# Weighing and scoring attention pair by pair, with the flags' reductions and first weight sums at other places

## The chip, the cores and the metric

The kernel runs on one core of a Trainium2 chip. A core has TensorE (PE, matmuls; its weight loads are shown as PEld), VectorE (DVE), ScalarE (ACT), GpSimd (POOL) and SyncE (SP, which here only issues DMAs). Each engine takes its instructions in the order in which the program lists them, and waits on semaphores for what others make. The metric is the device time of one execution in microseconds (us).

## The reference, cut to what matters

64 graphs of 256 nodes, 512 features each, pass through two layers of masked attention. All arithmetic is in float32.

```python
h = relu(layernorm(x))                       # layer 0: 4 heads of 64
q, k, v = h @ Wq, h @ Wk, h @ Wv
sim = where(adjacency, q @ k.T * 64**-0.5, -max)
x = x + softmax(sim) @ v @ Wo + bo
h = relu(layernorm(x))                       # layer 1: 8 heads of 64
h = layernorm(h) * gamma + beta
q, k, v = split(h @ w_qkv.T)
scores = where(adjacency | eye, q @ k.T * 64**-0.5, -1e9)
x = x + softmax(scores) @ v @ w_out.T + b_out
```

A node of layer 0 without any neighbour has all its scores masked alike, and its softmax is uniform. That is why the kernel needs a flag for each node, whether it has a neighbour at all: the maximum over its row of the adjacency.

## The kernel before, in words

**Steps and units.** Two graphs make a step; there are 32 (`NSTEP`). Heads go in pairs, since two heads of 64 fill 128 partitions. Layer 0 has the pairs 0 and 1 (called L0), layer 1 has 0 and 2 (L1A) and 1 and 3 (L1B). A set of two pairs is handled together.

**Matmuls of projections.** Every large product is cut into 2 x 2 blocks and done in 7 block products instead of 8. It needs sums of weight blocks (`weight_sum`, made once, at the start) and of activation blocks (`act_sums0`, `act_sums1`, on POOL). The products come in the order 1, 6, 5, 2, 7, 3, 4 (or 1, 5, 2, 6, 7, 3, 4). Products 2, 4 and 3 accumulate into the PSUM bank in which 1, 7 and 5 were left (`SHARED`), so they wait until that bank has been read. After each product VectorE or ScalarE takes the bank over (`evacuate`, L745 and on; `accumulate`, L764 and on).

**PSUM.** Eight banks: four with the name `sc` (pool `ps_sc`), and four `mm` banks, which `mm_tile` hands out in turn, the least recently used first, leaving out those held for a later product.

**A visit.** `visit(period, w, prev, cur)` is the piece of attention that stands between two blocks of projections. For the pairs of `prev`, `weigh_out` multiplies the exponentials by the values (L1041, 128x32 tiles of the array, four at a time), and ScalarE copies the result out (L1056). For the pairs of `cur`, `scores` makes the scores (L970, 64x128 tiles, two at a time), VectorE adds the mask while it moves them out (`mask_scores`, L993), and ScalarE takes exponentials (L998). Later POOL adds the two key halves (`key_halves`, L1005), VectorE turns and reduces them (L1011, L1018, `turn_sums` L1071, `key_sums` L1079 to L1083), the inverses go through DRAM by SP (L1089, L1100), and POOL multiplies the weighed values by them (`normalise`, L1116). With W for the weighing of a pair and S for its scores, TensorE does W0, W1, S0, S1. W0 and W1 write `sc` banks; S0 writes four `sc` banks; S1 writes two `mm` and two `sc` banks.

**The order.** It is written out by hand. `at(period, place, fn, ...)` files a piece of work under a number, period times 6.4 plus place, and at the end all pieces are sorted by it. Each engine gets its instructions in that order. `at_set` spreads the seven products of a projection over a length of one; a product's evacuation is filed just ahead of the next product. A period of the steady state, for step s:

| place | TensorE |
|---|---|
| 0.0 | queries and keys of L1A (`project_qk`, L817) |
| 1.0 | `combine` of layer 1 of the step before (L914) |
| 2.0 (`AT_X`) | visit X: weighs layer 0 of the next step, scores L1A |
| 2.0 | values of layer 1 (`project_v1`, L898); adjacency turned (L563) |
| 3.0 | `combine` of layer 0 of the next step (L914) |
| 3.5 | queries and keys of L1B (L817) |
| 4.5 (`AT_Q0`) | visit Q0: weighs L1A, scores L1B |
| 4.5 | queries and keys of layer 0, two steps ahead (L817) |
| 5.5 (`AT_V0`) | values of layer 0, turned (`project_v0_turned`, L864) |
| 6.2 (`AT_Z`) | visit Z: weighs L1B, scores layer 0 |

**Work beside it.** The adjacency flags are made by `neighbours` (VectorE, maximum, L521), `neighbours_line` (VectorE, four small transposes into one row, L530) and `neighbours_spread` (three DMAs from SP that copy the row, L537). `norm0` and `norm1` take the moments (L590, L591); POOL makes the scales (`row_scales`, L600 to L602); ScalarE applies them (L606). The normalised h is turned by VectorE in 32 x 32 blocks (`turn_blocks`, L700), moved by 16 DMAs (`move_blocks`, L712) and placed by ScalarE (`place_h`, L723 for layer 0, L725 for layer 1). The values of layer 0 are turned by `turn_values` (VectorE, L878) into a tile that `place_h` of layer 1 has to have read, and moved by ScalarE's queue (L888).

**x and its tiles.** The residual x of a step is loaded in two halves by ScalarE's queue (`load_graph`, L502) into one of two tiles, gets its biases from POOL (`first_bias` L508, `second_bias` L652), and is stored in two halves (`store_graph`, L948), the first graph by ScalarE's queue, the second by SP's. A tile is loaded anew only when both halves of the step before the last are stored. The load is filed at X + 0.005 and X + 0.025, the first pair's exponentials at X + 0.02 and X + 0.03.

Of the kernel before, what the change touches and what calls it, by code (L numbers as in the profile page):

```python
# [8 lines left out]
FP = mybir.dt.float32  # L9
# [306 lines left out]
def fast_path(  # L316
# [19 lines left out]
    nc = tc.nc  # L336
    P = 128
    B, N, D = x.shape
    DH = 64
    G = 2  # L340
    NSTEP = B // G
# [689 lines left out]
            st["oT0"] = flat[:, :NB].rearrange("p (b c) n -> p b c n", c=HP0)  # L1031
            st["invb"] = [flat[:, 8:10], flat[:, 10:12]]

    def weigh(s, lyr, pr):
        st = S[s]
        p = st["p", lyr, pr]
        po = ps_sc.tile([P, G, N], FP, name="sc")
        for g in range(G):
            for kc in range(NIC):
                for r0 in range(0, P, 32):  # L1040
                    nc.tensor.matmul(  # L1041
                        po[r0:r0 + 32, g, :],
                        (
                            st["v1"][:, g * NIC + kc, pr * P + r0:pr * P + r0 + Q] if lyr else
                            st["v0"][:, r0 // Q, pr, g * NIC + kc, :]
                        ),
                        p[r0 // DH][:, g, kc, :], start=(kc == 0), stop=(kc == NIC - 1),
                    )
        half = (HP0, HP1)[lyr]
        b0, b1, step = B_OF[pr // half]  # L1050
        dst = st[f"oT{lyr}"][:, b0:b1:step, pr % half, :]
        return po, dst

    def weigh_out(s, lyr, pr):
        po, dst = weigh(s, lyr, pr)
        nc.scalar.copy(dst, po)  # L1056
        S[s]["dst", lyr, pr] = dst

    def weigh_last(pr):

        po, dst = weigh(NSTEP - 1, 1, pr)
        nc.vector.tensor_tensor(dst, po, S[NSTEP - 1]["invb", 1, pr], ALU.mult)

    def turn_sums(s, lyr, prs):
# [78 lines left out]
    def visit(period, w, prev, cur):  # L1143

        w -= 0.0003
        s, lyr, prs = prev
        last = (s, lyr) == (NSTEP - 1, 1)
        if prs:
            if prs[0] == 0 and not last:
                at(period, w - 0.0002, place_values, s, lyr)  # L1150
            if (s, lyr) == (1, 0):
                turned = sums = 0, 0.88
            elif 0 <= period < NSTEP - 2 and s > 0:
                sums = turned = (
                    (period, AT_X + 1.45) if abs(w - AT_Q0) < 0.01 else
                    (period, AT_V0 + 0.5595) if abs(w - AT_Z) < 0.01 else (period - 1, AT_Z + 1.25)
                )
                if abs(w - AT_Z) < 0.01:
                    turned = period, AT_V0 + 0.41
            else:  # L1160
                turned = sums = period, w - 0.0001
            at(*turned, turn_sums, s, lyr, prs)
            at(*sums, key_sums, s, lyr, prs)
            at(period, w - 0.00008, inverse_in, s, lyr, prs)
            for i, pr in enumerate(prs):
                if not last:
                    at(period, w, weigh_out, s, lyr, pr)
                    at(period, w + (0.55 if len(prs) == 1 else (0.3, 0.75)[i]), normalise, s, lyr, pr)
        z, q = w > AT_Z - 0.01 and period < NSTEP - 2, abs(w - AT_Q0) < 0.01 and 0 <= period < NSTEP - 2
        for i, pr in enumerate(cur[2]):  # L1170
            unit = (*cur[:2], pr)
            one = cur[:2] == (0, 0)
            at(period, w, scores, *unit, i == 1)
            at(period, w, mask_scores, *unit, 0)
            at(period, w + 1 / 7 if one else w, mask_scores, *unit, 1)
            for g, place in enumerate((0.05, 0.22) if one else ((0.02, 0.03), (0.15, 0.3))[i]):
                at(period, w + place, exponentials, *unit, g)
            for e, place in enumerate((0.23, 0.3) if one else ((0.1, 0.11), (0.495, 0.496) if z else (0.435, 0.436) if q else (0.35, 0.36))[i]):
                if unit == (1, 0, 1):
                    at(0, 0.45 + place, key_halves, *unit, e)  # L1180
                else:
                    at(period, w + place, key_halves, *unit, e)
            if cur[:2] == (1, 0):
                period, w, key = 0, 0.0, (*cur[:2], (0, 1), pr)
                turn, add = ((0.44, 0.441), (0.715, 0.87))[pr]
            else:
                turn, add = (
                    ((0.31, 0.311), (0.6583, 0.6585))[pr] if one else ((0.49, 0.491), (0.63, 0.92))[i] if z else
                    ((0.43, 0.431), (1.02, 1.021))[i] if q else ((0.29, 0.291), (0.715, 1.001 if w < AT_X else 0.87))[i]
                )  # L1190
                key = (*cur, i)
            at(period, w + turn, turn_keys, cur[0])
            at(period, w + add, key_quarters, *key)
# [26 lines left out]
    for s in range(NSTEP):  # L1220
# [7 lines left out]
        for t in range(NT):  # L1228
            at(p, (0.5 + 0.4 * t, 1.95 + 0.1395 * t)[s] if s < 2 else (0.95, 1.05, 1.2, 1.35)[t], norm0, s, t)
            if s == 0:  # L1230
                at(p, 0.95 + 0.4 * t, first_scale, t)
            else:
                at(p, (2.6 + 0.1 * t, 2.35 + 0.001 * t)[s - 1] if s < 3 else 1.6 + 0.001 * t, scale_row, s, t)
            if not by_tensor(s, 0):
                at(p, AT_X - 0.00035 + 0.00001 * t if s > 2 else 2.9 + 0.03 * t, turn_blocks, s, 0, t)
        if not by_tensor(s, 0):
            at(p, AT_X - 0.00031 if s > 2 else 3.0, move_blocks, s)
        for g in range(G):
            at(p, (1.8, 2.7)[s] if s < 2 else (0.3 if s == 2 else 0.94) + 0.001 * g, neighbours, s, g)
        if s < 2:  # L1240
            at(p, (2.9, 2.72)[s], neighbours_rows, s)
            at(p, (FIRST_Q0 + 0.285, 3.59)[s], neighbours_turn, s)
        else:
            at(p, 0.31 if s == 2 else 0.945, neighbours_line, s)
            at(p, 0.32 if s == 2 else 0.946, neighbours_spread, s)
        at(p, (FIRST_Q0 + 0.1425, 3.583)[s] if s < 2 else 2.5, adjacency_turn, s)
        at(p, (FIRST_Q0 + 0.3, 3.74)[s] if s < 2 else 3.1, mask0, s)
        at(p, (FIRST_Q0 + 0.31, 4.43)[s] if s < 2 else 5.85, mask1, s)
# [12 lines left out]
        if s < 2:  # L1261
            for t in range(NT):
                place = (FIRST_V0 + 0.14 * t - (0 if t else 0.0005), (4.31, 5.02, 5.16, 5.31)[t])[s]
                at_dense(p, place, 0.14, project_v0, s, t)
        else:
            for i, n in enumerate(SET):
                at_dense(p, AT_V0 + 0.08 * i, 0.08, project_v0_turned, s, n)
            at(p, 6.13, turn_values, s)
            at(p, 6.6, move_values, s, 0)
            at(p, 6.98, move_values, s, 1)  # L1270
        p = s - 1
# [3 lines left out]
        if edge < 2:  # L1275
            at(p, (0.0, 0.2)[edge], load_x, s)
        else:
            at(p, AT_X + 0.005 if s > 1 else 1.2, load_graph, s, 1)
            at(p, AT_X + 0.025 if s > 1 else 1.2, load_graph, s, 0)
        for k, t in enumerate(NORM1):  # L1280
            at(p, (1.55, 1.5, (2.34, 2.5, 2.85, 2.86)[k])[edge], first_bias, s, t)
        if edge == 2:
# [9 lines left out]
        for k in range(NT):  # L1292
            at(p, ((2.901, 3.041, 3.181, 3.321), (2.99919, 2.99933, 2.99947, 2.99961), (3.79, 3.8, 3.94, 3.95))[edge][k], norm1, s, k)
            at(
                p, ((3.042, 3.182, 3.322, 3.323), (2.99948, 3.2, 3.3, 3.45), (4.08, 4.22, 4.23, 4.37))[edge][k],
                norm1_rest, s, k,
            )
            at(p, (9.38 + 0.001 * k, 6.5 + 0.1 * k, 5.6 + 0.01 * k)[edge], second_bias, s, k)
            place = ((3.6112, 3.6113, 3.7502, 3.7503)[k], 3.6 + 0.01 * k, AT_Q0 - 0.0002 + 0.00001 * k)[edge]
            at(p, place, scale_row, s, NORM1[k])  # L1300
            if edge == 2:
                at(p, AT_Q0 + (0.15, 0.16, 0.29, 0.3)[k], turn_blocks, s, 1, NORM1[k])
# [2 lines left out]

        turn = (3.763, 3.9995, AT_H1)[edge]
        for c in range(NC):
            at(p, turn + 0.00001 * c, transpose_h if edge < 2 else place_h, s, 1, c)
        at(p, turn + (0.001, 0.0001, 0.155)[edge], lambda s=s: act_sums0(S[s]["hT"]))
        at(p, turn + (0.002, 0.0001, 0.156)[edge], lambda s=s: act_sums1(S[s]["hT"]))  # L1310
        p = s
        if s < NSTEP - 1:
# [5 lines left out]
            at(p, place - 0.23, lambda s=s: act_sums1(S[s]["oT1"]))  # L1318
            at_set(p, place, SETC, combine, s, 1)
            at(p, place + 6 / 7 + 0.001, store_graph, s, 1)  # L1320
            at(p, place + 0.9994, store_graph, s, 0)
        else:
            p = s - 1
            at_set(p, LAST_QK, SET, project_qk, s, 1, 0)
# [28 lines left out]
    for i in range(4):  # L1353
        at(-1, 0.1 + 0.01 * i, weight_sum, nc.vector, wqkv1[:, :, :, 0, :], i)
        at(-1, 0.54 + 0.0001 * i, weight_sum, nc.gpsimd, wqkv1[:, :, :, 1, :], i)
        at(0, 0.65, weight_sum, nc.gpsimd, wqkv1[:, :, :, 2, :], i)
        at(0, (3.55, 3.6, 4.38, 4.4)[i], weight_sum, nc.gpsimd, wo1, i)
        at(0, 1.1, weight_sum, nc.gpsimd, wv0, i)
    for _, _, fn, args in sorted(events, key=lambda e: e[:2]):
        fn(*args)  # L1360

# [51 lines left out]
```

## Time and profile before

| what | us |
|---|---|
| median of 3 runs (lowest, highest) | 3152.93 (3152.81, 3155.26) |
| profiled execution, its own time | 3154.19 |
| its span, first to last instruction | 3152.2 |
| TensorE busy | 3102.9 (98%) |
| VectorE busy | 2439.1 (77%) |
| POOL busy | 2237.5 (71%) |
| ScalarE busy | 1223.6 (39%) |
| DMA, mean over the span | 80 GB/s |
| granted TensorE clock, mean | 0.999 |

Each engine's busy time is the union of its instructions. TensorE's matmuls overlap: one is shown with 0.38 us while the next begins 0.216 us after it, so that a late matmul costs more than the idle time shown ahead of it. Rows of the timeline merge equal instructions that follow each other ("x56"), and name in brackets the idle time of the engine before the row, with what ended it. Such a releaser is inferred: of several semaphores the one that came last by the profile is named.

### The profile page before, as it was taken

To read this page: it belongs to the slowest core of one execution; us is meant where nothing else is said; L and a number is where in the kernel's file an instruction comes from. 1 tells how busy PE (TensorE), PEld (TensorE's weight loads), DVE (VectorE), ACT (ScalarE), POOL (GpSimd) and SP (SyncE) were. 2 spreads that over 40 slices of the span, in tenths; PEclk is the share of its full clock that TensorE was granted. 3 is DMA by queue.
4 is the path that set the end of the run, shared out by engine and by line. 5 is a ranking of instruction groups with operands and counts; after the bars stand their busy time and mean duration, and the time that the engine had idled before them with its cause. 6 is when DMAs were issued, how large, how long until landed. Compare 5 with 4: busy or idle time off the path is not lost.

```text
span 3152.2 us, 55625 instructions
## 1 busy us (share of the span) xinstructions
PE 3102.9 (98%) x20362; PEld 2537.4 (80%) x20362; DVE 2439.1 (77%) x4371; ACT 1223.6 (39%) x2166; POOL 2237.5 (71%) x2128
## 2 busy tenths in 40 slices
PE   8999999999999999999999999999999999999998
PEld 6778878888888888888887888888888888888787
DVE  6778777777778787777777777777778777777766
ACT  4424444343433434343434334343334434343431
POOL 7876866767767777677677677776776866767753
PEclk9999999999999999999999999999999999999999
DMA  4232222332323323223222233132232222332311
GB/s 139 59 92 77 73 83 72 92 91 60 87 70 94 92 59 85 75 85 92 85 66 83 72 97 91 53 90 74 88 92 75 73 84 72 94 91 56 90 35 49
DMA packets 187591, 251.24 MB, mean 80 GB/s; under 512 B 58088, under 2 KB 78192, under 8 KB 187312
## 3 DMA queue, kind: packets, MB, share of 16 engines
q1 hardware_dynamic: 139088, 183.74, 20.5%
q10 hardware_dynamic: 48224, 63.87, 6.6%
q8 instruction: 164, 2.69, 0.4%
q14 instruction: 115, 0.94, 0.1%
HBM read 128.59 MB, written 34.34 MB: 52 GB/s over the span
## 4 chain that ended last, share of the span: by engine, by line
PE 62%; DVE 13%; POOL 12%; DMA 6%; issue 5%; SPq 1%; ACT 0%; ACTq 0%; POOLq 0%; DVEq 0%
PE mm L817 29%; PE sc L1041 8%; PE sc L970 7%; PE mm L864 6%; PE mm L914 5%; PE mm L898 4%; POOL pd L1005 3%; POOL xt L508 3%; DMA h<-blocks 3%; DMA out_dram<-xt 2%; DVE bs L590 2%; PE mm L970 2%; DMA xt<-in_x_dram 1%; DVE turned_p L1011 1%; POOL oT L1116 1%
## 5 line engine op out<-in xcount | busy, mean ns | idle before, releaser
L817 PE MATMUL mm<-hT,wqkv 128*128 128x256 f32 x3584 | 789.8, 381 | 0.5 <-ACT wo L471 0.5
L817 PEld LDWEIGHTS mm<-hT,wqkv 128*128 128x128 f32 x3584 | 678.9, 190 | 103.4 <-issue 12.1
L1005 POOL TENSOR_TENSOR pd<-p 128x512 f32<-128x512 f32 x383 | 479.5, 1274 | 369.5 <-ACT p L998 264.3
L914 PE MATMUL mm<-wo,oT 128*128 128x256 f32 x2632 | 595.0, 381 | 27.1 <-POOL mr L602 12.2
L914 PEld LDWEIGHTS mm<-wo,oT 128*128 128x128 f32 x2632 | 494.1, 190 | 118.3 <-POOL mr L601 23.0
L993 DVE TENSOR_TENSOR p<-sc,n 128x512 f32<-128x512 f32 x579 | 362.5, 681 | 176.8 <-PE sc L970 176.7
L998 ACT ACTIVATE p<-p 128x512 f32<-128x512 f32 x766 | 431.0, 623 | 156.2 <-DVE p L993 121.0
L898 PE MATMUL mm<-wqkv,hT 128*128 128x256 f32 x1792 | 402.3, 382 | 3.6 <-DVE v L755 3.2
L817 PE MATMUL mm<-hT,wqk 128*128 128x256 f32 x1792 | 398.0, 382 | 0.3 <-ACT qk L751 0.2
L817 PEld LDWEIGHTS mm<-hT,wqk 128*128 128x128 f32 x1792 | 338.0, 190 | 55.9 <-issue 10.3
L898 PEld LDWEIGHTS mm<-wqkv,hT 128*128 128x128 f32 x1792 | 335.4, 190 | 57.7 <-issue 10.3
L1041 PE MATMUL sc<-p,v 128*32 128x256 f32 x6128 | 351.4, 381 | 0.0
L1041 PEld LDWEIGHTS sc<-p,v 128*32 128x32 f32 x6128 | 189.7, 110 | 146.0 <-issue 31.2
L970 PE MATMUL sc<-qk 64*128 64x256 f32 x2320 | 294.7, 385 | 3.4 <-DVE p L993 3.4
L606 ACT ACTIVATE h<-h,mr,r 128x512 f32<-128x512 f32 x252 | 184.9, 805 | 247.4 <-POOL mr L602 247.4
L970 PEld LDWEIGHTS sc<-qk 64*128 64x128 f32 x2320 | 219.0, 186 | 64.4 <-issue 27.5
L1011 DVE STREAM_TRANSPOSE turned_p<-pd 128x1024 f32<-128x1024 f32 x192 | 237.1, 1235 | 38.6 <-POOL pd L1005 38.4
L1116 POOL TENSOR_TENSOR oT<-oT 128x512 f32<-128x512 f32 x188 | 239.8, 1276 | 0.0
L785 POOL TENSOR_TENSOR xt<-xt,u 128x512 f32<-128x512 f32 x183 | 229.2, 1273 | 12.2 <-DVE xt L779 9.5
L1018 DVE TENSOR_REDUCE part<-turned_p 128x32 f32<-128x1024 f32 x192 | 233.0, 1214 | 4.4
L864 PE MATMUL mm<-hT,wv 128*128 128x256 f32 x840 | 188.6, 382 | 0.0
L864 PEld LDWEIGHTS mm<-hT,wv 128*128 128x128 f32 x840 | 156.6, 190 | 27.1 <-ACT vT L751 6.1
(150 smaller groups left out, 4015.6 us busy)
## 6 DMA issues: line engine op xcount, KB each, us to landing
h<-blocks SPq DMA_DIRECT2D x960, 64.0 KB, 2.0
oT<-line SPq DMA_DIRECT2D x376, 128.0 KB, 3.1
h<-in_x_dram SPq DMA_DIRECT2D x31, 1024.0 KB, 7.5
xt<-in_x_dram ACTq DMA_DIRECT2D x60, 512.0 KB, 5.9
out_dram<-xt SPq DMA_DIRECT2D x31, 512.0 KB, 3.3
out_dram<-xt ACTq DMA_DIRECT2D x31, 512.0 KB, 4.5
v<-values ACTq DMA_DIRECT2D x480, 32.0 KB, 1.9
ne<-ne SPq DMA_DIRECT2D x90, 64.0 KB, 2.0
```

The source lines that it names most:

```text
L817: nc.tensor.matmul(bank[:, k, :], w[:, wa, c, k, a * P:(a + 1) * P], st["hT"][:, ba, c, :], start=first and (k, c) == (0, 0), stop=(k, c) ...
L864: nc.tensor.matmul(bank, wv0[:, wa, c, :], st["hT"][:, ba, c, :], start=first and c == 0, stop=c == HC - 1, skip_group_check=True,)
L898: nc.tensor.matmul(bank[:, t, :], st["hT"][:, ba, c, t * P:(t + 1) * P], wqkv1[:, wa, c, 2, :], start=first and (t, c) == (0, 0), stop=(t, ...
L914: nc.tensor.matmul(bank[:, t, :], oT[:, ba, c, t * P:(t + 1) * P], w[:, wa, c, :], start=first and (t, c) == (0, 0), stop=(t, c) == (NIC - ...
L970: nc.tensor.matmul(sc[g][e][:, kc, :], qk[rows, 1, k0:k0 + P], qk[rows, 0, g * N:(g + 1) * N], start=True, stop=True,)
L993: nc.vector.tensor_tensor(p[e][:, g], sc[e], neg[:, :, g, :], ALU.add)
L998: nc.scalar.activation(p[e][:, g], p[e][:, g], AF.Exp, scale=SCALE)
L1005: nc.gpsimd.tensor_tensor(st["pd"][:, e], p[e][:, :, 0, :], p[e][:, :, 1, :], ALU.add)
L1011: nc.vector.transpose(st["turned_p"], st.pop("pd").rearrange("p e g (b k) -> p (e g b) k", k=32))
L1018: nc.vector.tensor_reduce(st["part", lyr, prs][:, i], st.pop("turned_p"), axis=mybir.AxisListType.X, op=ALU.add)
L1041: nc.tensor.matmul(po[r0:r0 + 32, g, :], (st["v1"][:, g * NIC + kc, pr * P + r0:pr * P + r0 + Q] if lyr else st["v0"][:, r0 // Q, pr, g * ...
L1116: nc.gpsimd.tensor_tensor(dst, dst, invb, ALU.mult)
```

## The change

What is computed stays as it is. Moved are:

- *Visits.* W0 S0 W1 S1 in place of W0 W1 S0 S1: the second pair's pieces are filed 0.0002 later. The second pair is weighed into an `mm` bank. The first pair's exponentials are filed at +0.00015 and +0.00016 in visits with two pairs, ahead of the second pair's copy, and ahead of the loads of x in X.
- *Flags.* From step 3 on, the maximum goes from place 0.94 (just ahead of the combine of layer 1) to just ahead of Q0 in the period before; the row and its DMAs go from 0.945 to 0.05, just behind Z. Step 2 has places of its own.
- *Around Z.* The second half of layer 1's `place_h` is filed behind the first pair's copy; `turn_values` behind the first pair's masks.
- *Around X.* ScalarE's store of the first graph is filed behind the first pair's copy (0.99975 for 0.9994); the load of the first graph directly behind that of the second.
- *Start.* POOL's sums of `wv0` go from 1.1 to 3.61 in the first period, those of `wo1` from 3.55, 3.6, 4.38, 4.4 to 4.7 (three) and 5.55; step 0's second bias goes to 3.6; step 2's h is turned earlier; the key sums of step 0 in layer 1 get the places that all other steps have.

```diff
-    def weigh(s, lyr, pr):
+    def weigh(s, lyr, pr, second):
-        po = ps_sc.tile([P, G, N], FP, name="sc")
+        po = mm_tile([P, G, N]) if second else ps_sc.tile([P, G, N], FP, name="sc")
...
-            elif 0 <= period < NSTEP - 2 and s > 0:
+            elif 0 <= period < NSTEP - 2:
                 sums = turned = (
...
-                    at(period, w, weigh_out, s, lyr, pr)
+                    at(period, w + 0.0002 * i, weigh_out, s, lyr, pr, i == 1)
...
-            at(period, w, scores, *unit, i == 1)
-            at(period, w, mask_scores, *unit, 0)
-            at(period, w + 1 / 7 if one else w, mask_scores, *unit, 1)
-            for g, place in enumerate((0.05, 0.22) if one else ((0.02, 0.03), (0.15, 0.3))[i]):
+            at(period, w + 0.0002 * i, scores, *unit, i == 1)
+            at(period, w + 0.0002 * i, mask_scores, *unit, 0)
+            at(period, w + 1 / 7 if one else w + 0.0002 * i, mask_scores, *unit, 1)
+            both = len(cur[2]) == 2
+            for g, place in enumerate((0.05, 0.22) if one else ((0.00015, 0.00016) if both else (0.02, 0.03), (0.15, 0.3))[i]):
                 at(period, w + place, exponentials, *unit, g)
...
-                at(p, AT_X - 0.00035 + 0.00001 * t if s > 2 else 2.9 + 0.03 * t, turn_blocks, s, 0, t)
+                at(p, AT_X - 0.00035 + 0.00001 * t if s > 2 else (2.6, 2.601, 2.72, 2.721)[t], turn_blocks, s, 0, t)
...
-            at(p, (1.8, 2.7)[s] if s < 2 else (0.3 if s == 2 else 0.94) + 0.001 * g, neighbours, s, g)
+            if s < 3:
+                at(p, (1.8, 2.7, 0.1)[s] + 0.001 * g, neighbours, s, g)
+            else:
+                at(p - 1, AT_Q0 - 0.0009, neighbours, s, g)
...
-            at(p, 0.31 if s == 2 else 0.945, neighbours_line, s)
-            at(p, 0.32 if s == 2 else 0.946, neighbours_spread, s)
+            at(p, 2.3 if s == 2 else 0.05, neighbours_line, s)
+            at(p, 2.31 if s == 2 else 0.051, neighbours_spread, s)
...
-            at(p, 6.13, turn_values, s)
+            at(p, AT_Z - 0.0002, turn_values, s)
...
-            at(p, AT_X + 0.025 if s > 1 else 1.2, load_graph, s, 0)
+            at(p, AT_X + 0.0051 if s > 1 else 1.2, load_graph, s, 0)
...
-            at(p, (9.38 + 0.001 * k, 6.5 + 0.1 * k, 5.6 + 0.01 * k)[edge], second_bias, s, k)
+            at(*((0, 3.6 + 0.001 * k), (p, 6.5 + 0.1 * k), (p, 5.6 + 0.01 * k))[edge], second_bias, s, k)
...
-            at(p, turn + 0.00001 * c, transpose_h if edge < 2 else place_h, s, 1, c)
+            at(
+                p, turn + 0.00001 * c if edge < 2 or c < HC else AT_Z - 0.00029 + 0.00001 * c,
+                transpose_h if edge < 2 else place_h, s, 1, c,
+            )
...
-            at(p, place + 0.9994, store_graph, s, 0)
+            at(p, place + (0.99975 if s < NSTEP - 2 else 0.9994), store_graph, s, 0)
...
-        at(0, (3.55, 3.6, 4.38, 4.4)[i], weight_sum, nc.gpsimd, wo1, i)
-        at(0, 1.1, weight_sum, nc.gpsimd, wv0, i)
+        at(0, (4.7, 4.701, 4.702, 5.55)[i], weight_sum, nc.gpsimd, wo1, i)
+        at(0, 3.61, weight_sum, nc.gpsimd, wv0, i)
```

More of the change, by code (lines that the diff above doesn't have):

```diff
@@ L1052, in weigh, with weigh_out @@
         return po, dst
-    def weigh_out(s, lyr, pr):
-        po, dst = weigh(s, lyr, pr)
+    def weigh_out(s, lyr, pr, second):
+        po, dst = weigh(s, lyr, pr, second)
         nc.scalar.copy(dst, po)
@@ L1059, in weigh_last @@
     def weigh_last(pr):
-        po, dst = weigh(NSTEP - 1, 1, pr)
+        po, dst = weigh(NSTEP - 1, 1, pr, False)
         nc.vector.tensor_tensor(dst, po, S[NSTEP - 1]["invb", 1, pr], ALU.mult)
```

## The prediction

> **What bounds the kernel.** I read the engine table first, then TensorE's waits, then the timeline of TensorE in one period (96.3 us from one visit X to the next), then of the engines that hold it up.
>
> The page's engine table:
> ```profile
> PE 3102.9 (98%) x20362; PEld 2537.4 (80%) x20362; DVE 2439.1 (77%) x4371; ACT 1223.6 (39%) x2166; POOL 2237.5 (71%) x2128
> ```
> TensorE (PE) is the bound; the others matter only where it waits for them, or where its own stream is broken up. The table of TensorE's waits (total us, times, longest):
> ```profile
> PE mm L914 <- POOL mr L602: 12.2, 29, 0.4
> PE mm L914 <- DVE xt L774: 11.6, 23, 0.7
> ...
> PE sc L970 <- DVE p L993: 3.4, 3, 1.5
> PE mm L898 <- DVE v L755: 3.2, 1, 3.2
> PE mm L914 <- POOL oT L408: 3.0, 4, 1.1
> ```
> L914 is `combine`. Its first row is layer 1's, its second layer 0's, always at product 4, which accumulates into the bank that product 7 has left. What one such wait costs, and what a visit costs, stands in TensorE's timeline of a period (start, length, line, number):
> ```profile
> 1069.71 10.52 PE L914 MATMUL mm<-wo,oT 128*128 128x256 f32 x48
> 1080.66 1.97 PE L914 MATMUL mm<-wo,oT 128*128 128x256 f32 x8 [0.43 <-POOL mr L602]
> 1082.55 3.66 PE L1041 MATMUL sc<-p,v 128*32 128x256 f32 x64
> 1086.14 2.00 PE L970 MATMUL sc<-qk 64*128 64x256 f32 x16
> ...
> 1089.80 0.48 PE L898 MATMUL mm<-wqkv,hT 128*128 128x256 f32 x1
> ```
> Combine takes 12.84 from its first start to the next block's. Near the end, where no flags are reduced beside it, the same 56 matmuls run from 3004.03 to 3016.20, 12.17. So the wait costs 0.66, more than the 0.43 shown, since matmuls overlap. The named releaser (POOL's L602) has nothing to do with this bank; VectorE's order tells why it is late:
> ```profile
> 1069.33 1.26 DVE L521 TENSOR_REDUCE any_of<-ad 128x2 f32<-128x512 uint8 x2
> 1070.62 1.24 DVE L530 STREAM_TRANSPOSE ne<-any_of 32x128 f32<-32x128 f32 x4
> ...
> 1079.83 0.68 DVE L774 TENSOR_TENSOR xt<-mm,xt 128x512 f32<-128x512 f32 x1
> ```
> The last is product 7's addition. Its matmuls were through by 1078.5, it starts at 1079.83 because VectorE is still working off its queue, and TensorE goes on 0.15 after its end. The 2.50 us in the first two rows are the flags' maximum and row.
>
> A visit is 3.59 of weighing (1082.55 to 1086.14) and 3.66 of scores (to 1089.80): 7.25. What it is in halves is seen at the start, where visits have one pair:
> ```profile
> 39.31 1.93 PE L1041 MATMUL sc<-p,v 128*32 128x256 f32 x32
> 41.17 2.00 PE L970 MATMUL sc<-qk 64*128 64x256 f32 x16
> 43.10 1.99 PE L817 MATMUL mm<-hT,wqk 128*128 128x256 f32 x8
> ```
> Half a weighing is 1.86, not 1.80, and half the scores 1.93, not 1.83.
>
> **What the skill says.** The Trainium skill, TensorEngine Tiling (Array Packing), Tiling Modes, says that changing the tiling mode drains TensorE. The trace agrees: weighing is 128x32, scores 64x128, the rest 128x128, and each change costs 0.13 to 0.20 (3.59 and 3.66 against 16 x 0.216 = 3.46; 0.216 is the distance of matmuls inside a block). The skill's page TensorE: Matmul & The Clock Gate, Part 1, says that the clock falls to half after a window without enough work. The trace agrees once: after a wait of 1.54 at 179.5 the granted clock is 0.55 from 181.0 to 184.5. The same page, Architectural detail, says that VectorE and ScalarE take instructions strictly in order, as all rows above show. The skill's page DMA: Bandwidth & Descriptors, Anatomy of one DMA, says that the end of a write to HBM is told late; here the store issued by ScalarE at 405.17 has landed at 410.8, and a load waits for it.
>
> **The change, part by part.**
>
> *Visits pair by pair.* W0 W1 S0 S1 becomes W0 S0 W1 S1: two more changes of mode. By the half visits 2 x (1.86 + 1.93) = 7.58 against 7.25: +0.33. The program has 93 visits with two pairs on both sides (31 X, 30 Q0, 30 Z, 2 at the end): 93 x 0.33 = **+30.7**. Scores followed directly by weighing stand nowhere in the trace. From below the switch is free (0.33 - 0.13 = 0.20 a visit, +18.6), from above it costs as much as the dearer switch (0.40, +37). I take 0.33, as a switch seems to cost the drain and the load of the new weights, whatever went before.
>
> W1 now writes one of the four `mm` banks. It is the least recently used, free before all three kinds of visit. The next stage's second product needs it back 9.3 us after the visit's start (7.58, and 1.73 for the first product). Its copy stands on ScalarE behind four exponentials: in Q0, the fullest, 4 placements of h (2.19), the first copy (0.56), 4 scalings (2.93), 4 exponentials (2.19) and the copy (0.59) end 8.5 after the start. Hidden, with 0.8 left. S0's last bank is W0's: its copy ends 2.7 after the start in Q0 and S0 comes to it at 2.9: free, or 0.05 to 0.1 with the semaphore, **+1.5** for 30 visits.
>
> *The flags' maximum and row.* The maximum (1.26) goes ahead of Q0's masks, where VectorE waits over 2 for scores; the row (1.24) behind Z's masks, ahead of the first addition, 3.7 after the visit: there VectorE was idle for 1.45. Both are covered, and the row's three DMAs move with it on SP, behind Z's loads of inverses, ahead of the loads of flags, with no one waiting. Combine's queue is 2.50 shorter, its lateness was about 1.1: the wait ends, 29 x 0.66 = **-19.1**.
>
> *Exponentials ahead of loads in X.* Layer 0's combine takes 6.29 in the clean periods (6 of 30), and 206.0 in all 30 (start to start by the timeline): 17.3 above 30 x 6.29, 0.25 of wait being in each of the 6.29. What makes a period bad is read from ScalarE and POOL:
> ```profile
> 410.96 0.38 ACTq L502 DMA_DIRECT2D xt<-in_x_dram  x1
> 411.45 0.63 ACT L998 ACTIVATE p<-p 128x512 f32<-128x512 f32 x1 [4.16 <-DVE p L993]
> 413.19 1.27 POOL L1005 TENSOR_TENSOR pd<-p 128x512 f32<-128x512 f32 x1 [8.05 <-ACT p L998]
> ```
> ScalarE's queue waits at the load of the next x (L502) until the store has freed the tile, the exponentials wait behind it, and POOL starts its chain (key halves, normalisation, first biases, combine's sums) 10.15 after the visit's start; at 1082.55 it was 8.3 and combine was clean. Afterwards the exponentials come first: masks from 3.1, the exponentials' end at 6.2, POOL from 5.7. The loads then go out at 6.8, or 8.3 in bad periods (the store is behind a copy, +0.4). Near 2927 the load took 4.2: it lands at 11.0 to 12.5. POOL reaches its first bias at 9.5 and waits for that; before, it got there at 12.0 to 13.8. The key halves of the second pair then start at 12.3 to 13.8, less 0.33 for the longer visit, where 13.4 still was clean. I take back 16 of the 17.3: **-16**. The bounds are -17.3, and 0 if the loads land as late as the chain came before.
>
> *Start.* In the first period POOL no longer does the second bias (4.95) and the first sums of wv (3.14) ahead of X's key halves, and VectorE has the row's 1.24 less. That removes the wait of 3.4 at 118.7, and the late masks at 107.6 (1.8). At 179.5 VectorE's key sums came behind Z's `turn_values`; moved, they free the masks (2.4), and the clock stays up (1.7). Another 0.8 at 94 stood behind the row. Together 10.1; moved POOL work (8.1 us at 3.6, 3.95 in Q0) fits its gaps up to some 2 us, so **-8.5** (bounds -10.1 and -2).
>
> The second half of h's placement, `turn_values` and the store move by some us behind pair 0's work; covered by the 1.9 of W1, and 0.
>
> Sum: 3152.2 + 30.7 + 1.5 - 19.1 - 16 - 8.5 = 3140.8. The profiled execution took 3154.19, 2.0 more than its span; the runs' median is 1.26 below that. So 3140.8 + 0.7 = **3141.5**, 11.4 faster.
>
> **Rivals.**
> 1. *The copy of W1 is late* (the slower side). Place: ScalarE in Q0, where the second product of layer 0's projection waits for its bank. It decides from 0.8 us of lateness beyond my count; each further 0.6 costs 30 x 0.6 = 18: 3159.5. For it: ScalarE's queue was not so deep before. Against: 0.8 of slack, and all durations come from rows.
> 2. *POOL's chain gains nothing*, as the loads now stand behind the copy and the first bias waits for them: combine of layer 0 stays at 17.3, the start keeps 2: 3141.5 + 16 + 2 = 3159.5 at worst, 3151 if half is lost. For it: loads go out up to 0.8 later than now.
> 3. *Switches are cheaper* (0.20 a visit): 3129.
> 4. *The waits only change place*: POOL's L602 is the true releaser in layer 1's combine, so 19.1 stays: 3160. Against: resumption follows L774 by 0.15 in that combine and in layer 0's.
>
> **Numbers.** My sum 0.60 (3136 to 3147); rival 1 0.12, rival 2 0.14, rival 3 0.08, rival 4 0.06. Changes of 0.2% (6.3 us) can be told from none. Faster (under 3146.6): most of the sum, rival 3: 0.65. Within: its upper edge and the milder half of rival 2: 0.18. Slower: rivals 1 and 4, the worst of 2: 0.17. The range, 3132 to 3161, leaves out the cheapest switches and two mishaps together.
>
> **What will show it.** In the profile after: a two-pair visit of 7.58 (7.45 if the switch from scores to weighing is free); no L914 row of 29 waits; L914 behind L774 about 0.25 a period (less than 8 in all), no POOL oT L408; no waits over 1 us between 90 and 190; PEclk whole at 181. Wrong if TensorE has a new row of some 30 waits (for ScalarE's L1056, or L1041 itself), or if L508 on POOL waits for L502's DMA longer than to 13 us after X.

## The result, and the profile after

The changed kernel takes 3144.15 us (median of 8 runs, 3143.20 to 3145.02); the kernel before, run beside it, 3153.99 (8 runs, 3152.81 to 3156.13). The ratio is 0.9968, 95% interval [0.9957, 0.9979]: about 10 us faster. The profiled execution took 3143.63, its span is 3141.5 (before: 3152.2), so the span became 10.7 shorter.

The engine table of the kernel after:
```profile
PE 3125.5 (99%) x20362; PEld 2524.9 (80%) x20362; DVE 2462.6 (78%) x4371; ACT 1218.3 (39%) x2166; POOL 2244.6 (71%) x2128
```
TensorE is busy 22.6 longer than before (3125.5 against 3102.9) while the span is 10.7 shorter: the same 20362 matmuls take more time, and TensorE's idle time has fallen from 49.3 to 16.0. Both halves of the change are in this one line. The table of TensorE's waits after (total us, times, longest), complete:
```profile
PE mm L734 <- ACT h L632: 7.0, 3, 6.5
PE sc L970 <- DVE p L993: 1.4, 2, 0.9
PE mm L847 <- DVE qk L761: 0.4, 1, 0.4
PE mm L898 <- ACT v L751: 0.4, 1, 0.4
```
Both rows of `combine` (L914), 12.2 in 29 waits and 11.6 in 23, have left the table, with the 3.2 of the values (L898) and the 3.0 behind POOL. What stays, L734, belongs to the first matmuls of the program, which wait for the first h; before they had 7.3.

TensorE's timeline, one combine of layer 1 and the visit X after it (start, length, engine, line, tiles, number):
```profile
1056.91 12.25 PE L914 MATMUL mm<-wo,oT 128*128 128x256 f32 x56
1069.10 1.93 PE L1041 MATMUL sc<-p,v 128*32 128x256 f32 x32
1070.96 2.00 PE L970 MATMUL sc<-qk 64*128 64x256 f32 x16
1072.89 1.93 PE L1041 MATMUL mm<-p,v 128*32 128x256 f32 x32
1074.75 1.14 PE L970 MATMUL mm<-qk 64*128 64x256 f32 x8
...
1076.68 6.53 PE L898 MATMUL mm<-wqkv,hT 128*128 128x256 f32 x29
```
Combine is one row of 56, without the break after the 48th that it had before, and takes 12.19 from its start to the next block's. The visit goes from 1069.10 to 1076.68: 7.58, in four pieces of 1.86, 1.93, 1.86 and 1.93, where it took 7.25 before.

VectorE in the same period, at the three places that the flags concern:
```profile
1011.98 1.27 DVE L521 TENSOR_REDUCE any_of<-ad 128x2 f32<-128x512 uint8 x2
1014.10 2.48 DVE L993 TENSOR_TENSOR p<-sc,n 128x512 f32<-128x512 f32 x4 [0.86 <-PE sc L970]
...
1046.36 1.23 DVE L530 STREAM_TRANSPOSE ne<-any_of 32x128 f32<-32x128 f32 x4
1048.55 0.69 DVE L753 TENSOR_TENSOR qk<-mm,qk 128x512 f32<-128x512 f32 x1 [0.96 <-PE mm L817]
...
1065.75 0.69 DVE L774 TENSOR_TENSOR xt<-mm,xt 128x512 f32<-128x512 f32 x1 [1.04 <-PE mm L914]
```
The maximum now stands ahead of Q0's masks and the row ahead of the first addition behind Z. After each of them VectorE still waits (0.86, 0.96) for TensorE, so neither costs anything. The last line is product 7's addition: VectorE now waits for TensorE there (1.04), where before TensorE waited for VectorE. It is over at 1066.44; product 4 comes to the bank at 1056.91 + 48 x 0.2157 = 1067.26.

In the same step as the rows shown of before, ScalarE's visit X (from 391.70):
```profile
395.57 2.37 ACT L998 ACTIVATE p<-p 128x512 f32<-128x512 f32 x4 [1.28 <-DVE p L993]
397.84 0.57 ACT L1056 COPY oT<-mm 128x512 f32<-128x512 f32 x1
398.26 2.60 ACTq L502 DMA_DIRECT2D xt<-in_x_dram  x2
```
and POOL beside it:
```profile
397.41 2.51 POOL L1005 TENSOR_TENSOR pd<-p 128x512 f32<-128x512 f32 x2 [3.55 <-ACT p L998]
399.87 1.28 POOL L1116 TENSOR_TENSOR oT<-oT 128x512 f32<-128x512 f32 x1
402.72 1.27 POOL L508 TENSOR_TENSOR xt<-xt,bo_b 128x512 f32<-128x512 f32 x1 [1.57 <-DMA xt<-in_x_dram]
405.10 1.27 POOL L1005 TENSOR_TENSOR pd<-p 128x512 f32<-128x512 f32 x1 [1.11 <-DVE turned_p L1011]
```
The exponentials stand ahead of the loads, POOL starts its key halves 5.71 after the visit's start in every steady period (8.3 to 10.2 before, where a load follows). It then waits for the load at the first bias (L508), as foretold, and here still has 1.11 to spare before the second pair's key halves.

**Where the 10.7 went**, from TensorE's timeline, block by block, each from its start to the start of the next:

| | said | measured |
|---|---|---|
| two more changes of tiling in 93 visits | +30.7 | +31.7 |
| Q0: first scores wait for a bank (30 x 0.08) | +1.5 | +2.4 |
| 29 late combines of layer 1 | -19.1 | -19.1 |
| 30 combines of layer 0 (206.0 to 188.9) | -16 | -17.1 |
| the start | -8.5 | -8.6 |
| sum | -11.4 | -10.7 |

The first row is worked out: all weighings grew by 12.8 and all scores by 18.35; from this the 2.4 of Q0 are taken, and 2.9 are added, by which two late scores at the start became less late (they are counted in the row of the start): 31.7, or 0.34 a visit. All other blocks together differ by less than 0.5. The row of the start is not the work of the start's moves alone: with the visits alone (below) the scores of the first Z are in time too (2.4) and the clock stays whole behind them. Either part is enough for these two terms.

### The profile page after: what moved, and what is told of

Its sections match the earlier page's. It is cut to its first block, busy times and chain, and to the rows that moved or that the text cites. A ratio compares the mean times of both kernels' runs of the same rounds, so it can differ in the third digit from the quotient of the medians.

```text
span 3141.5 us, 55627 instructions
## 1 busy us (share of the span) xinstructions
PE 3125.5 (99%) x20362; PEld 2524.9 (80%) x20362; DVE 2462.6 (78%) x4371; ACT 1218.3 (39%) x2166; POOL 2244.6 (71%) x2128
## 4 chain that ended last, share of the span: by engine, by line
PE 98%; DVE 1%; POOL 1%; DMA 0%; ACT 0%; issue 0%; SPq 0%; ACTq 0%; DVEq 0%; POOLq 0%
PE mm L817 37%; PE mm L914 18%; PE mm L898 12%; PE sc L970 9%; PE mm L864 6%; PE sc L1041 6%; PE mm L1041 5%; PE mm L970 3%; PE mm L847 1%; PE mm L563 0%; PE mm L940 0%; PE mm L466 0%; PE mm L675 0%; POOL pd L1005 0%; POOL wqk L652 0%
## 5 line engine op out<-in xcount | busy, mean ns | idle before, releaser
L914 PE MATMUL mm<-wo,oT 128*128 128x256 f32 x2632 | 585.5, 380 | 0.5
L914 PEld LDWEIGHTS mm<-wo,oT 128*128 128x128 f32 x2632 | 497.4, 190 | 78.7 <-issue 11.5
L898 PE MATMUL mm<-wqkv,hT 128*128 128x256 f32 x1792 | 402.1, 382 | 0.4 <-ACT v L751 0.4
L898 PEld LDWEIGHTS mm<-wqkv,hT 128*128 128x128 f32 x1792 | 335.5, 190 | 54.2 <-issue 10.3
L508 POOL TENSOR_TENSOR xt<-xt,bo_b 128x512 f32<-128x512 f32 x124 | 156.3, 1273 | 56.2 <-DMA xt<-in_x_dram 50.9
L1041 PE MATMUL sc<-p,v 128*32 128x256 f32 x3152 | 190.8, 382 | 0.0
L993 DVE TENSOR_TENSOR p<-mm,n 128x512 f32<-128x512 f32 x187 | 120.4, 686 | 85.9 <-PE mm L970 85.9
```

The source lines that it names most:

```text
L898: nc.tensor.matmul(bank[:, t, :], st["hT"][:, ba, c, t * P:(t + 1) * P], wqkv1[:, wa, c, 2, :], start=first and (t, c) == (0, 0), stop=(t, ...
L914: nc.tensor.matmul(bank[:, t, :], oT[:, ba, c, t * P:(t + 1) * P], w[:, wa, c, :], start=first and (t, c) == (0, 0), stop=(t, c) == (NIC - ...
L993: nc.vector.tensor_tensor(p[e][:, g], sc[e], neg[:, :, g, :], ALU.add)
L1041: nc.tensor.matmul(po[r0:r0 + 32, g, :], (st["v1"][:, g * NIC + kc, pr * P + r0:pr * P + r0 + Q] if lyr else st["v0"][:, r0 // Q, pr, g * ...
```

## The experiments

### The visits alone

The kernel before with all that belongs to the pairs: the order W0 S0 W1 S1, the bank of W1, the exponentials ahead of copy and loads, `turn_values`, the placement, the store and the load of the first graph. Flags and start stay. Two of its lines:

```diff
-                    at(period, w, weigh_out, s, lyr, pr)
+                    at(period, w + 0.0002 * i, weigh_out, s, lyr, pr, i == 1)
...
-            at(period, w, scores, *unit, i == 1)
+            at(period, w + 0.0002 * i, scores, *unit, i == 1)
```

> The kernel before with the visits alone in pairs (weighing into an mm bank, exponentials ahead of the loads, second half of the placement, turning of values, store and load as in the change); flags and start as before. My theory, that each of 93 visits pays two more mode switches: two-pair visits of 7.58 us, +31.6, and +2.4 for the late bank in Q0; layer 0's combine back to 6.29 each, -17; the two late masks at the start -4; layer 1's combine keeps its 0.66: about 3154 + 13 = 3167. Rival, that the switches cost nothing net because the pairs keep VectorE and ScalarE busy earlier: 3154 - 21 = 3133, with visits of 7.25.

Measured: 3170.02 (3169.33 to 3170.56) against 3153.23 (8 runs, 3151.89 to 3156.38), ratio 1.0053 [1.0036, 1.0070]. TensorE's waits in that kernel:
```profile
PE mm L914 <- POOL mr L602: 12.3, 29, 0.4
...
PE mm L914 <- DVE xt L774: 1.3, 2, 0.7
```
Weighing grew by 12.8 and scores by 18.6. Layer 1's waits stay all 29; layer 0's row fell from 11.6 to 1.3, worth 14.3. So the pairs by themselves make the kernel 17 us slower. They bring the 14 in layer 0's combines, and the weighings and scores grow by 31; in this sum the two late scores at the start, 2.9 less late, are already taken off.

### The flags alone

```diff
-            at(p, (1.8, 2.7)[s] if s < 2 else (0.3 if s == 2 else 0.94) + 0.001 * g, neighbours, s, g)
+            if s < 3:
+                at(p, (1.8, 2.7, 0.1)[s] + 0.001 * g, neighbours, s, g)
+            else:
+                at(p - 1, AT_Q0 - 0.0009, neighbours, s, g)
...
-            at(p, 0.31 if s == 2 else 0.945, neighbours_line, s)
-            at(p, 0.32 if s == 2 else 0.946, neighbours_spread, s)
+            at(p, 2.3 if s == 2 else 0.05, neighbours_line, s)
+            at(p, 2.31 if s == 2 else 0.051, neighbours_spread, s)
```

> The kernel before with the flags' maximum and row alone at their new places. My theory, that 2.50 us of VectorE's queue ahead of combine are what makes product 7's addition late: the 29 waits in layer 1's combine go, -19, time 3135. Rival, that POOL's scales (L602) release them, or that the wait moves to the next product: 3154, with the row of 29 waits still there.

Measured: 3132.98 (3130.95 to 3134.64), ratio 0.9936 [0.9919, 0.9953], on the same chip as the visits alone. TensorE's waits:
```profile
PE mm L914 <- DVE xt L774: 9.6, 20, 0.7
...
PE mm L898 <- DVE v L755: 3.8, 1, 3.8
```
and VectorE around product 7 of that kernel's combine:
```profile
1069.38 0.69 DVE L772 TENSOR_TENSOR u<-mm,u 128x512 f32<-128x512 f32 x1
1071.11 0.69 DVE L774 TENSOR_TENSOR xt<-mm,xt 128x512 f32<-128x512 f32 x1 [1.04 <-PE mm L914]
```
The row of 29 is gone, the combines of layer 1 are 19.1 shorter, and layer 0's row stays, as it should (its combines are 4.4 shorter in all). This alone does not clear POOL's L602 of the wait: the statistics that it needs stand in the same queue of VectorE, so that it too comes earlier. The trace of the kernel before clears it: in all 29 waits product 4 begins 0.146 to 0.147 after the end of L774, as it does in layer 0's combine, where no L602 is near, and it begins 2 to 6 ns before L602 has ended. L602 was named since it ended within some ns of the wait. So VectorE's queue was the cause, and rival 4 falls.

### The loads alone

Only the two loads of x are filed behind the first pair's exponentials; the visits stay as before.

```diff
-            at(p, AT_X + 0.005 if s > 1 else 1.2, load_graph, s, 1)
-            at(p, AT_X + 0.025 if s > 1 else 1.2, load_graph, s, 0)
+            at(p, AT_X + 0.035 if s > 1 else 1.2, load_graph, s, 1)
+            at(p, AT_X + 0.0351 if s > 1 else 1.2, load_graph, s, 0)
```

> The kernel before with the two loads of x alone behind the first pair's exponentials (at X + 0.035). My theory, that POOL's chain is late because ScalarE's queue stands at the load: POOL's key halves begin near 7.4 us after X in every period, loads land near 12.3, layer 0's combine loses about 0.1 to 0.2 over its 6.29: -12, time 3142. Rival, that the first bias waits for the load just as long: no gain, 3154, with POOL idle ahead of L508.

Measured: 3141.92 (3139.12 to 3142.92), ratio 0.9961 [0.9947, 0.9975], same chip. TensorE's waits:
```profile
PE mm L914 <- POOL mr L602: 12.2, 29, 0.4
...
PE mm L914 <- DVE xt L774: 1.0, 3, 0.4
```
ScalarE in its visit X (from 1076.03):
```profile
1081.57 2.36 ACT L998 ACTIVATE p<-p 128x512 f32<-128x512 f32 x4 [1.23 <-DVE p L993]
1083.40 1.15 ACTq L502 DMA_DIRECT2D xt<-in_x_dram  x2
```
POOL's key halves start 7.38 after the visit's start in every period, and the combines of layer 0 are clean but for three: the first, at the start of the program, and the two where the load came latest. There the first bias starts 12.77 and 12.58 after the visit's start, and the combine is 0.43 and 0.26 longer. All 30 together are 16.2 shorter. So the 14 to 17 that the pairs gave layer 0 need no pairs: only the place of two DMA issues. The time fell by 11.3 and not by 16; 1.7 of the difference is a stretch at half clock behind the first values' wait at 119, which the kernel before does not have there, and the profiled execution, from which the 16.2 come, was 2.2 below the median.

### The start alone

The kernel before with the places of `weight_sum`, `second_bias` of step 0, `turn_blocks` of step 2 and step 0's key sums, all as in the diff of the change.

> The kernel before with only the moves of the start (POOL's sums of wv0 and wo1 and step 0's second bias later, step 2's turning of h earlier, step 0's key sums at the place of all other steps). My theory: the first products of the values no longer wait for their weight sums (-3.4), the first combine of layer 0 is no longer late (-2.0), the masks at 179 come in time (-2.4) and the clock stays up after them (-1.7): about -9, so 3144 to 3145 where the kernel before has 3153.2. Periods after the first stay as before, so the rows of 29 and of some 20 waits of combine remain. The rival: the work that POOL puts off comes due at another wait, 3152 to 3156.

Measured: 3145.76 (11 runs, 3143.81 to 3150.35) against 3153.08 (14 runs, 3149.74 to 3155.75), ratio 0.9978 [0.9969, 0.9987]: 7.3 less, where 9 was expected. The values lost their 3.4, the first combine of layer 0 its 2.0, Z's scores their 2.4, and the half clock is gone; the rows of 29 and 20 waits stand. TensorE's timeline behind Z, though:
```profile
173.06 1.03 PE L970 MATMUL sc<-qk 64*128 64x256 f32 x8
174.02 8.90 PE L817 MATMUL mm<-hT,wqkv 128*128 128x256 f32 x40
183.08 1.99 PE L817 MATMUL mm<-hT,wqkv 128*128 128x256 f32 x8 [0.16 <-DVE qk L755]
185.81 1.97 PE L817 MATMUL mm<-hT,wqkv 128*128 128x256 f32 x8 [0.74 <-DVE qk L757]
```
The block is broken twice by waits for VectorE, 1.4 together, that neither the kernel before nor the changed one has. The rival was right for this piece: here the end of one wait opened another. In the changed kernel the same block is a single row of 56, 12.37 from its start to the next block's. The kernel without pairs (below), which has flags, loads and start, still has both breaks (0.19 and 0.74), and the visits alone have none. So what removes them is in the visits' part, which also moves `turn_values` behind the first masks; that move alone was not tried.

### All but the pairs

Flags, start and loads together, with the visits of before (W0 W1 S0 S1).

> The changed kernel with its visits back in the old order (W0 W1 S0 S1, all weighing in sc banks, placement, turning and store as before), loads behind the first pair's exponentials; flags and start as in the change. My theory, that the pairs only cost: visits of 7.25, -31.6 - 2.4 against the change, +3 for layer 0's combine and late first masks: about 3144 - 31 = 3113. Rival, that the pairs are what feeds VectorE, ScalarE and POOL early enough: the waits come back and it stays at 3135 or more.

Measured: 3113.82 (3111.77 to 3114.49), ratio 0.9875 [0.9859, 0.9892]; on another chip 3113.58, ratio 0.9875 [0.9858, 0.9891]:

> The same kernel without pairs once more, beside the one with the other order of products on the same chip: 3113.8 within 2.

TensorE's waits at combine have shrunk to one row:
```profile
PE mm L914 <- DVE xt L774: 0.4, 2, 0.2
```
Its combines take the same time as those of the changed kernel (389.8 for the blocks of layer 1 in both, 189.2 and 188.9 for those of layer 0), its scores and weighings are 33.5 shorter. So the moves give about 39, and with the pairs, as the change was made, about 30 of it are paid back. The pairs do give one thing, a little more cover for late loads: with the visits alone a first bias at 12.57 after the visit's start cost the combine nothing, where with the loads alone one at 12.58 cost 0.26. In the second set of runs without pairs the combines of layer 0 took 191.5 in the profile, 2.2 more, for such loads.

### Each block of both pairs cut once more

Weighing and scores cut graph by graph: eight blocks in a two-pair visit where the changed kernel has four.

```diff
-                    at(period, w + 0.0002 * i, weigh_out, s, lyr, pr, i == 1)
+                    if len(prs) == 2 and len(cur[2]) == 2:
+                        at(period, w + 0.0002 * i, weigh_out, s, lyr, pr, i == 1, (0,))
+                        at(period, w + 0.0002 * i + 0.000002, weigh_out, s, lyr, pr, i == 1, (1,))
...
-            at(period, w + 0.0002 * i, scores, *unit, i == 1)
...
+                at(period, w + 0.0002 * i + 0.000001, scores, *unit, i == 1, (0,))
+                at(period, w + 0.0002 * i + 0.000003, scores, *unit, i == 1, (1,))
```

> The changed kernel with the weighing and the scores of each pair cut once more, graph by graph (W S W S W S W S, each half as long), in the 93 visits with two pairs: four more changes of tiling per visit. If a change of tiling has a fixed price whatever the length of the blocks, as I take it (0.33 us for one more weighing and one more scores block), a visit takes 7.58 + 0.66 = 8.24 and the program 93 x 0.66 = 61 more than the changed kernel: 3205. The rival: the price belongs to long blocks (weights loaded ahead, data waited for), or a change back to weighing costs nothing: at 0.20 for each pair of blocks 93 x 0.40 = 37, 3181; with no price for short blocks 3144.

Measured: 3276.63 (3276.11 to 3277.16), 132 above the changed kernel, where 61 was expected: a miss. TensorE's timeline of one visit of it (here weighing is L1046, scores L971, the copy L1063):
```profile
1110.46 1.07 PE L1046 MATMUL sc<-p,v 128*32 128x256 f32 x16
1111.46 1.13 PE L971 MATMUL sc<-qk 64*128 64x256 f32 x8
1112.52 1.07 PE L1046 MATMUL sc<-p,v 128*32 128x256 f32 x16
1113.52 1.93 PE L971 MATMUL sc<-qk 64*128 64x256 f32 x8
1115.38 1.07 PE L1046 MATMUL mm<-p,v 128*32 128x256 f32 x16
1116.38 1.13 PE L971 MATMUL mm<-qk 64*128 64x256 f32 x8
```
Half a weighing takes 1.00 in all cases, half the scores 1.06, but one half of the scores in each visit 1.86. This last is the first pair's second half: it needs the bank of W0, which ScalarE copies out only after W0's second half, and that half now stands directly ahead of it. ScalarE at the same place:
```profile
1113.69 0.58 ACT L1063 COPY oT<-sc 128x512 f32<-128x512 f32 x1 [4.04 <-PE sc L1046]
```
The copy ends at 1114.27, and the first matmul into that bank starts at 1114.32. So 0.80 x 93, about 74, is a wait that this edit made itself, and the changes of tiling cost the rest: 4 x (1.00 + 1.06) - 7.58 = 0.66 a visit, 61 (the 2.4 that the changed kernel waits in Q0 anyway are in the 74). To have it without that wait, one more run was made.

### Only the second pair cut once more

The same cut for W1 and S1 alone, whose banks are free.

> The changed kernel with only the second pair of each two-pair visit cut graph by graph (W S W S W S, the first two full, the last four half as long). The cut of all four blocks cost 132, of which by the blocks 92 x 0.80 was a wait of my own making: the second half of the first pair's scores needs the bank from which ScalarE still copies the first weighing out. The second pair's scores take mm banks and two sc banks that the masks have left, so that wait should be gone. Theory of a fixed price for each change of tiling: a half of weighing takes 1.00 and a half of scores 1.06, so the visit is 2 x (1.00 + 1.06) - (1.86 + 1.93) = 0.33 longer, 93 x 0.33 = 31 in all: 3172 to 3176. The rival, that changes between short blocks cost more than between long ones (the 132 of the full cut shared by two): 3210. A price of 0.20 would give 3162.

Measured: 3176.23 (3175.72 to 3176.67) against 3152.91 (7 runs, 3151.45 to 3155.09), ratio 1.0073 [1.0057, 1.0090]. It is 32 above the changed kernel, just over the upper edge of what was expected. TensorE's timeline of its second pair:
```profile
1083.15 1.07 PE L1046 MATMUL mm<-p,v 128*32 128x256 f32 x16
1084.15 1.13 PE L971 MATMUL mm<-qk 64*128 64x256 f32 x8
1085.21 1.07 PE L1046 MATMUL mm<-p,v 128*32 128x256 f32 x16
1086.21 1.13 PE L971 MATMUL sc<-qk 64*128 64x256 f32 x8
1087.28 5.01 PE L898 MATMUL mm<-wqkv,hT 128*128 128x256 f32 x22
```
4.13 against 3.79 for the uncut pair, all weighings and scores together 31.06 more: one more weighing and scores block costs 0.33 again, though the blocks are half as long. The price is one for each change, not one for the work. It is not one for each new block either: in the kernel of the last experiment combine is followed by a block of the same full tiles, and the matmuls at that border start 0.217 apart, as inside a block. This agrees with the Trainium skill (TensorEngine Tiling (Array Packing), Tiling Modes), which says that a change of mode drains TensorE.

### The other order of products

The combine of layer 0 keeps a wait of 0.25 for product 7's bank in all kernels so far. In the kernel without pairs, product 7 is made one place earlier, in this combine and in the values of layer 0:

```diff
-    SETC0 = (1, 6, 5, 2, 7, 3, 4)
+    SETC0 = (1, 6, 5, 7, 2, 3, 4)
```

> The changed kernel with the visits of before (both weighings, then both scores), and in the combine of layer 0 and in the values of layer 0 the products in the order 1, 6, 5, 7, 2, 3, 4, so that product 4 comes two products after the one that leaves it its bank, in place of one and a half. The kernel without pairs took 3113.8. If the 0.25 us in each of 30 combines of layer 0 is the wait for that bank alone: 30 x 0.25 = 7.5 less, and some 2 us less in the values: 3104 to 3106. The rival: product 2 or 3 now waits in its place, 3113 to 3116.

Measured: 3102.98 (3102.70 to 3103.70), ratio 0.9843 [0.9826, 0.9859], beside the kernel without pairs at 3113.58 on the same chip: 10.6 less. TensorE's timeline:
```profile
1077.40 6.21 PE L914 MATMUL mm<-wo,oT 128*128 128x256 f32 x28
1083.45 12.25 PE L817 MATMUL mm<-hT,wqkv 128*128 128x256 f32 x56
```
Combine of layer 0 takes 6.05 where it took 6.29, in 30 places 7.9 less (189.2 to 181.3, against the first set of runs without pairs), and the values of layer 0 are 2.0 less. No other product waits instead, and the time is 1 below what was expected. This is the fastest of all versions run, 50 us under the kernel before.

## Why the prediction was right

It said 3141.5, in a range from 3132 to 3161; measured are 3144.15. Step by step:

- *Visits pair by pair.* The step took the price of a visit from the half visits at the start, 2 x (1.86 + 1.93). The blocks after are these to the hundredth, and the visit is 7.58 as foretold. Rival 3 (a cheaper change from scores to weighing) fell: its 7.45 doesn't appear, and the cut of the second pair gives 0.33 once more. That the drain and a load of new weights make up the price was only argued; the runs show how large it is, and that it comes with the change of tiling.
- *The bank of S0 in Q0.* Said 0.05 to 0.1; in all 30 visits the first scores take 2.01 for 1.93: 0.08. *The copy of W1* in Q0 ends 8.15 after the visit's start (1018.65 + 0.58 against 1011.08; said 8.5), before the second product needs the bank at 9.3, and no wait shows: rival 1 fell.
- *The flags.* Right in place and size, and the flags alone showed it: 29 x 0.66.
- *Exponentials ahead of loads.* Said -16, measured -17.1: only one combine of the 30 shows a wait (0.14) beside the common 0.25. POOL was to start from 5.7 after the visit's start; it starts at 5.71 (the 10.15 of the bad period is 10.2 when it is counted in the same way). Rival 2 had a true half: POOL does wait for the load at the first bias, in all 29 periods, 56.2 in all (for 27 of them, 50.9, the profile names the load). But it starts that bias at 10.6 to 12.8 after the visit's start, and the second key halves, which come next, wait for VectorE until 13.40 anyway: in 26 of the 29 periods they start then. In two they are late because of the load, at 13.49 and 14.00; a third, at 13.75, has an early load (bias at 11.3), and its cause stays open. The wait is covered, but for the one combine. With the loads alone the bias starts at 11.6 to 12.8, and the cover is used up in the two latest.
- *The start.* Said -8.5, measured -8.6, but not by the same terms. The values (3.4), Z's masks (2.4), the clock (1.5 of 1.7) and the wait at 94 (0.8) went as said. The scores at 104 stay late: of 1.8, only 0.5 went, for ahead of their masks VectorE still has four statistics of the norm (up to 106.43), not the row that the step took for the cause. The step had left 1.6 out because POOL's moved work might not fit; that this covered another miss, and the sum agrees to 0.1, is luck.
- *The clock.* The step read the half clock at 181 as what follows a wait of 1.54. The wait alone does not decide it: the kernel before waits 3.19 at 118.7 and keeps its full clock, and the flags alone wait 1.56 at the same place as the 1.54 and keep it too. That removing the wait kept the clock whole came true, but the reason is open.
- *From the span to the time.* The sum gave a span of 3140.8, measured are 3141.5. The step from there to the runs took 0.7; it is 2.65 here. The term was mis-sized, mostly since the median of before came from three runs: in eight it is 3153.99, 1.8 above the span. The remaining 0.85 is within the spread of runs of one kernel.

So the mechanisms stood, but for the late scores at 104 and the rule read into the clock. The terms were out by up to 1.1 each, in part against each other. The time was missed by 2.65: 0.7 from the sum, 1.95 from the step to the runs.

## What to carry to other kernels

A change of the array's tiling costs TensorE a fixed time (here 0.33 for one more weighing and one more scores block), so blocks of one tiling are kept together, and work that is to come earlier is moved on the engine that is late, not by cutting TensorE's blocks. A wait of TensorE at an accumulation is followed back to the queue of the engine that empties the bank: short work that nobody waits for yet (a flag, a row) or an issue of DMA that waits for a store is moved out of it, and where that isn't possible the product that needs the bank is made later. Take a change apart before it is kept: here one part took back three quarters of what the others gave.

## What was not expected of the hardware

- The price depends on where the change leads: 0.12 into the weighing's 128x32 tiles, from full tiles and from 64x128 alike; 0.21 into 64x128 from the weighing, and 0.20 from 64x128 back to full tiles. This is how much later than 0.216 after its predecessor the first matmul of the new tiling ends, in the kernel before and in the changed one alike. One more weighing and one more scores block so cost 0.12 + 0.21 = 0.33. What makes the difference was not tried.
- A wait of TensorE costs more than the idle time in its row: 0.43 shown, 0.66 gone when the wait was removed, 29 times over. The trace accounts for it: the matmul that waited starts 0.805 after its predecessor, where 0.216 is usual (0.59 more), and the one behind it starts 0.291 after it (0.075 more).
- The length of a wait does not tell whether the clock falls behind it. A wait of 3.2 at 119 left the granted clock at 1.00 in the kernel before and with the visits alone; with the loads alone the same wait of 3.2 was followed by 3.41 us at 0.5, and with the flags alone one of 3.8 was. A wait of 1.5 to 1.6 at 180 was followed by 3.41 us at 0.5 in the kernel before and with the loads alone, but not with the flags alone. What decides it was not found; a forecast does well to take such a stretch, worth 1.7 here, as chance.
- The loads of x, 0.5 MB each (256 x 512 float32), take 3.7 to 7.6 from issue to landing (median 5.3, 60 loads) in one and the same kernel, the changed one. A cover for such a load has to be sized by the late ones: in the loads' run it was the two latest that reached TensorE.
